# Attention in a fused block kernel: one running sum over all eight key blocks, a third buffer of upper keys, and four projections per area in halves

## The chip, the cores and the metric

The kernel runs on one core of one Trainium2 chip. The metric is the device time of one execution in microseconds. The core has a matrix engine (PE, with its weight loads shown apart as PEld), a vector engine (DVE), an activation engine (ACT), a general engine (POOL) and a queue engine (SP). ACT, POOL and SP can issue DMAs, which 16 DMA engines carry out. SBUF is the on-chip memory of 128 partitions; PSUM is the memory of eight banks per partition that PE writes.

## The reference, cut to what matters

The whole computation has two layers (an attention, a recurrence, convolutions with a state-space mixer, and a mixture of experts). The change touches the first part of layer 0 only, an attention over areas of the image. B = 2 images of 64 x 64 pixels with 256 channels are cut into four areas each; an area has 1024 pixels, and eight heads of 32 channels.

```python
qk = _conv1x1_bn(x, w_qk, qk_g, qk_b, qk_m, qk_v)
vv = _conv1x1_bn(x, w_v, v_g, v_b, v_m, v_v)
pp = conv_general_dilated(vv, w_pe, (1, 1), [(2, 2), (2, 2)], feature_group_count=C)
pp = _bn(pp, pe_g, pe_b, pe_m, pe_v)
...
attn = jnp.einsum('bhdn,bhdm->bhnm', q, k) * hd ** (-0.5)
attn = jax.nn.softmax(attn, axis=-1)
o = jnp.einsum('bhdm,bhnm->bhdn', v, attn)
...
return _conv1x1_bn(o + pp, w_proj, pr_g, pr_b, pr_m, pr_v)
```

The input of it is x, normalised over its channels, and the result is added to x. All is float32.

## The kernel before

**Tiling.** Eight areas (two images of four areas) are worked on one after the other. An area A has two groups of four heads, c = 0 and 1, so there are 16 groups G. A group has 1024 queries in two query halves n of 512, and 1024 keys in eight key blocks m of 128. The loop at L572 runs over 256 slots: slot t of a group (0 to 15) is query half n = t // 8 and key block m = t % 8. In tiles the four heads of a group lie on the 128 partitions for queries and keys (32 each).

**One slot** consists of, in the order in which the instructions are issued:

1. `scores` (L376): four matmuls of a bfloat16 row that subtracts each query's maximum (L381), then four matmuls of keys against queries (L386), into two PSUM tiles of two banks each. ACT takes the exponential of both into `exs[0]` and `exs[1]`, 128 x 1024 float32 each (L393). For m % 4 = 0 these tiles are named `sx0`, `sx1`, for the others `ex0`, `ex1`; each name has two buffers.
2. `values` (L403) of the slot before: four matmuls of the values against the exponentials (L399, `av_o`), summed over the eight key blocks in one PSUM bank.
3. `maxima` (L280) for the next group: four matmuls (L286). At even places ACT keeps the positive part of a product with the difference of upper and lower keys (`kd`, L298); at odd places DVE adds the product with the lower keys and takes the extreme value (L302), so that 1024 keys are searched in two products of 512.
4. The sum of exponentials, which the softmax divides by. It is not made from single key blocks: blocks are first added up on the 128 keys of a block. `total` is the pair of tiles of a block with m % 4 = 0. For the other blocks POOL issues a DMA that adds `exs[0]` into `total[0]` (L596); of `exs[1]` blocks 1 and 3 go by such a DMA (L602) and block 2 is added by POOL itself (L598), ordered behind the last matmul of `maxima` in that slot.
5. Other work of the same or neighbouring groups, from the tables `BEFORE`, `BEHIND`, `BEHIND_AREA`, `LATE` and `LATE_AREA` (L512 to L537), which name for each t a function, how many groups or areas ahead it works, and its arguments. `TAPS` says how many taps of the 5 x 5 depthwise convolution DVE does in each slot (L356).
6. Three slots after the fourth block of such a sum, `sums` (L414): four matmuls with a matrix of ones (L399, `po<-sx`) add up the 128 keys. After blocks 0 to 3 ACT keeps the result in `sum` (L421). After blocks 4 to 7 DVE adds `sum` and the new result (L425), turns it (L427), takes the reciprocal (L429), turns it back (L430) and multiplies the values (L433).

**Work from the tables** that the change moves: `query`, `key` (L260, L265: two matmuls of 512 columns by `project`, L157, and an ACT eviction with scale and bias), `v_half` (L227: the same for the values' image, and for half 0 two copies of border rows by POOL, L238 and L239), `v_tokens` (L241: four transposes on PE, one ACT copy), `output` (L366: projection and a DVE addition into x, L369), `mean_of_sum` and `variance_of_sum` (one 512-column product each, L172, and an ACT copy), `shift`, `centre`, `square`. Not moved are `root` (L203: at t = 6 a DVE transposition, at t = 7 POOL's power -0.5, L212 and L213), `join` (L308: four small POOL operations on the maxima, L318 and L319, at t = 11 and 15), `place` (L322: one matmul, an ACT copy, four DMAs from SP, L333, at t = 3 and 14) and `key_difference` (L271, at t = 15, L274).

**Order.** The order on every engine is the order of the program text (a manual schedule); the framework adds the semaphores that data and buffers need. A DMA that adds into a tile is issued by POOL after the DMA before it into the same tile has landed. PSUM has three tiles of two banks (`wide`, for scores and maxima), one bank `po` that all table work and the sums share, one use per slot, and one bank for `av_o`.

```python
tiles, k = [wide(), wide()], ks[G, m // HM]
...
exs.append(pe.tile([P, 2, 512], F32, name=f"{'ex' if m % 4 else 'sx'}{i}", bufs=2))
```

Of the kernel before, what the change touches and what calls it, by code (L numbers as in the profile page):

```python
# [10 lines left out]
F32 = mybir.dt.float32  # L11
# [3 lines left out]
ALU = mybir.AluOpType  # L15
# [3 lines left out]
P = 128  # L19
# [74 lines left out]
def area_attention(tc, sh, ap):  # L94
# [13 lines left out]
    with ExitStack() as ctx:  # L108
# [48 lines left out]
        def project(wt, c, src, half, out):  # L157

            for k in range(2):
                nc.tensor.matmul(  # L160
                    out, wt[:, k, c * P : (c + 1) * P], src(k)[:, HALVES[half]], start=k == 0, stop=k == 1
                )
# [61 lines left out]
        def columns(t):  # L224
            return lambda k: t[:, k]

        def v_half(A, c, half):  # L227

            if A not in vhs:
                vhs[A] = p2.tile([P, 2, AROWS + 4, WW], F32, name="vh")  # L230
            ps, r0 = bank(), 2 + half * AROWS // NQ
            project(w["wv"], c, columns(xns[A]), half, ps)
# [19 lines left out]
        def rows_of(wt, G, half, name, s, t, ps):  # L252
            A, c = GROUPS[G]
            ps = bank() if ps is None else ps
            project(wt, c, columns(xns[A]), half, ps)
            out = p2.tile([P, 512], F32, name=f"{name}{half}")
            nc.scalar.activation(out, ps, AF.Identity, scale=s[:, c : c + 1], bias=t[:, c : c + 1])
            return out

        def query(G, half, ps=None):  # L260
            if half == 0:
                nms[G] = p2.tile([P, NQ, GH, NM], F32, name="nm")
            qs[G, half] = rows_of(w["wq"], G, half, "q", s_qk, t_qk, ps)

        def key(G, half, ps=None):  # L265
            ks[G, half] = rows_of(w["wk"], G, half, "k", s_qk[:, 2:4], t_qk[:, 2:4], ps)
# [99 lines left out]
        def output(A, co, half):  # L366
            ps, to = bank(), area(A)[:, co, HALVES[half]]
            project(w["wpr"], co, lambda k: ys[A, k], half, ps)
            nc.vector.scalar_tensor_tensor(to, ps, s_pr[:, co : co + 1], to, ALU.mult, ALU.add)  # L369
# [6 lines left out]
        def scores(G, n, m):  # L376
# [37 lines left out]
        def sums(G, n, half, exs):  # L414
# [4 lines left out]
            if half == 0:  # L419
# [17 lines left out]
        with ExitStack() as own:  # L437
# [36 lines left out]
            query(0, 0, wide()[:, 0])  # L474
# [28 lines left out]
            for c in range(2):  # L503
# [10 lines left out]
            {0: [(1, query, 1)], 11: [(2, query, 0)], 13: [(2, key, 0)], 15: [(2, key, 1)]},  # L514
            {5: [(1, query, 1)], 9: [(2, query, 0)], 13: [(2, key, 0)], 15: [(2, key, 1)]},
# [16 lines left out]
                0: [(1, centre, 0)], 1: [(1, centre, 1), (1, square, 0)], 2: [(1, square, 1)],  # L532
# [7 lines left out]
        BEHIND_FIRST = {**BEHIND[0], 0: [(1, key, 1)]}  # L540
# [6 lines left out]
        for t in range(16):  # L547
# [3 lines left out]
            [2, 0, 1, 1, 2, 2, 2, 1, 2, 0, 0, 2, 3, 2, 3, 0],  # L551
            [4, 1, 1, 1, 3, 2, 3, 2, 2, 1, 1, 2, 2, 1, 2, 0],
# [19 lines left out]
        for g in range(16 * len(GROUPS)):  # L572
# [20 lines left out]
            if m % 4 == 0:  # L593
                total = exs
            if m % 4:
                nc.gpsimd.dma_start(total[0], exs[0], accum_op=ALU.add)  # L596
            if m % 4 == 3:
# [9 lines left out]
            works(G, t, BEHIND_FIRST if new else BEHIND[c], BEHIND_AREA[c])  # L607
# [7 lines left out]
            if m % 4 == 3:  # L615
                due[g + 3] = G, n, m // 4, total
# [1715 lines left out]
```

## Time and profile before

| | us |
|---|---|
| median of 3 runs (lowest, highest) | 2897.39 (2895.99, 2899.67) |
| the profiled execution | 2893.63 |
| span of its trace | 2891.8 |

| engine | busy us | share of the span | instructions |
|---|---|---|---|
| PE | 2631.5 | 91% | 17234 |
| PEld | 1483.3 | 51% | 17234 |
| DVE | 1963.8 | 68% | 3729 |
| ACT | 1554.5 | 54% | 2641 |
| POOL | 1239.8 | 43% | 1164 |

The rest of the profile is a page with slices of the span (each digit is the busy share of one fortieth of the span in tenths; PEclk is the granted clock of PE), the DMA queues, the chain of work that ended last, groups of instructions by line with their busy time and mean duration, and DMA issues. The trace behind it gives the order of time, the waits with what released them, and sums over stretches. In a row of the order of time stand start and duration in us, engine, line, operation, `out<-in`, shapes and a count; in brackets the idle time of the engine before it and what ended it. One float32 matmul of the program appears as two passes (x8 for four).

The groups that the change touches, each with count, busy us and mean ns: L596 DMA issue x192, 166.7, 868; L598 POOL addition x64, 171.8, 2684; ACT exponentials L393 `ex` x384, 376.1, 1029. In the chain that ended last, `PE po L399` has 2% of the span and `DMA sx<-ex` 3%. The queue of POOL's DMAs (q0) had its packets for 43.0% of 16 engines' span, and `sx<-ex` was issued 320 times with 512 KB each.

### The profile page before, as it was taken

The page shows a single profiled execution, that of the slowest core. Times are in us where ns is not written, and L with a number is a line of the kernel's source. Part 1 is how long each engine was busy: PE and PEld are TensorE (multiplying, and loading weights), DVE is VectorE, ACT ScalarE, POOL GpSimd, SP SyncE. Part 2 cuts the span into 40 slices and gives each one's busy share as a digit, 9 for nine tenths or more (in the row PEclk, how much of TensorE's full clock was granted, in tenths as well). Part 3 has the DMA queues.
Part 4 walks back from the last instruction along what each step waited for, and adds up shares of the span by engine and source line. Part 5 has one row for each costly group of instructions (what it writes and reads, how often), then busy time and mean ns, then how long its engine had stood idle before and what let it go on. Part 6 is the DMA issues. An engine that isn't in the chain of part 4 may idle for free.

```text
span 2891.8 us, 45886 instructions
## 1 busy us (share of the span) xinstructions
PE 2631.5 (91%) x17234; PEld 1483.3 (51%) x17234; DVE 1963.8 (68%) x3729; ACT 1554.5 (54%) x2641; POOL 1239.8 (43%) x1164
## 2 busy tenths in 40 slices
PE   7899999999999999997799999878885699999984
PEld 2223333333333333321699999833443588888873
DVE  5788879898888979786566667788887522222116
ACT  3567676666767676763344555576645522222223
POOL 1444545444444445443221000078771266666651
PEclk9999999999999999998899999989998899999995
DMA  3566666666676666767240000035553266666648
GB/s 132 110 128 126 129 128 131 126 132 131 128 137 132 132 132 127 138 130 144 90 175 1 2 1 1 9 99 150 142 136 122 87 235 221 229 225 227 229 171 342
DMA packets 104826, 388.16 MB, mean 134 GB/s; under 512 B 19656, under 2 KB 20560, under 8 KB 94864
## 3 DMA queue, kind: packets, MB, share of 16 engines
q0 software_dynamic: 71488, 293.00, 43.0%
q1 hardware_dynamic: 31872, 87.86, 9.4%
q10 hardware_dynamic: 1232, 4.25, 0.4%
q8 instruction: 138, 2.26, 0.3%
q14 instruction: 96, 0.79, 0.1%
HBM read 173.30 MB, written 43.58 MB: 75 GB/s over the span
## 4 chain that ended last, share of the span: by engine, by line
PE 73%; DVE 11%; issue 5%; DMA 4%; ACT 3%; POOL 3%; SPq 0%; ACTq 0%; DVEq 0%; POOLq 0%
PE ps L286 9%; PE ph L2078 9%; PE py L2088 8%; PE po L160 7%; PE av_o L399 7%; PE z L805 7%; PE z L817 7%; PE ps L386 6%; DMA sx<-ex 3%; PE ps L381 3%; PE yp L1560 2%; PE po L399 2%; DVE hs L1550 2%; DVE more L302 1%; DVE acc L356 1%
## 5 line engine op out<-in xcount | busy, mean ns | idle before, releaser
L356 DVE SCALAR_TENSOR_TENSOR acc<-vh,w_pe,acc 128x1008 f32<-128x1008 f32 (+7 forms) x384 | 529.5, 1382 | 9.1
L596 POOL DMA_DIRECT2D sx<-ex x192 | 166.7, 868 | 692.7 <-DMA sx<-ex 278.3
L393 ACT ACTIVATE ex<-ps 128x1024 f32<-128x1024 f32 x384 | 376.1, 1029 | 125.9 <-PE ps L386 50.4
L302 DVE CUSTOM_DVE_ANT_0 more<-ps,more 128x512 f32<-128x512 f32 x480 | 302.9, 687 | 133.5 <-PE ps L286 124.6
L2080 ACT ACTIVATE act<-ph,wt 128x256 f32<-128x256 f32 x272 | 128.8, 474 | 386.5 <-PE ph L2078 379.1
L2068 DVE COPY xt<-px 128x512 f32<-128x512 f32 x68 | 47.0, 692 | 396.5 <-PE px L2066 396.5
L2078 PE MATMUL ph<-xt,wt 128*128 128x256 f32 x1088 | 291.6, 391 | 5.0 <-ACT act L2080 3.0
L386 PE MATMUL ps<-q,k 32*128 32x512 f32 x2048 | 285.2, 602 | 0.0
L2088 PE MATMUL py<-wt,act 128*128 128x256 f32 x1088 | 278.7, 379 | 0.0
L298 ACT ACTIVATE more<-ps 128x1024 f32<-128x1024 f32 x240 | 233.4, 1028 | 26.8 <-issue 9.1
L2078 PEld LDWEIGHTS ph<-xt,wt 128*128 128x128 f32 x1088 | 190.4, 191 | 68.0 <-DVE xt L2068 24.0
L805 PE MATMUL z<-xs,u 128*128 128x128 f32 x1872 | 224.0, 277 | 0.0
L805 PEld LDWEIGHTS z<-xs,u 128*128 128x128 f32 x1872 | 217.7, 194 | 0.2 <-issue 0.2
L829 ACT ACTIVATE t<-z,bias 128x128 f32<-128x128 f32 x468 | 136.3, 361 | 145.1 <-PE z L817 145.1
L399 PE MATMUL av_o<-ex,vt 128*32 128x512 f32 x1536 | 212.0, 613 | 2.4 <-ACT ex L393 2.4
L2088 PEld LDWEIGHTS py<-wt,act 128*128 128x128 f32 x1088 | 201.6, 190 | 24.7
L2103 POOL DMA_INDIRECT results<-y,ri x136 | 138.0, 1014 | 138.9 <-DVE y L2096 115.6
L286 PE MATMUL ps<-k,q 32*128 32x512 f32 x1088 | 182.6, 639 | 1.7 <-DVE nm L292 1.3
L817 PE MATMUL z<-xs,v 128*128 128x128 f32 x1512 | 180.0, 275 | 0.1
L817 PEld LDWEIGHTS z<-xs,v 128*128 128x128 f32 x1512 | 174.2, 192 | 0.7 <-DVE xs L836 0.7
L598 POOL TENSOR_TENSOR sx<-sx,ex 128x1024 f32<-128x1024 f32 x64 | 171.8, 2684 | 4.7 <-PE ps L286 4.7
L1557 POOL TENSOR_TENSOR cs<-hs,cs 128x1024 f32<-128x1024 f32 x63 | 149.0, 2367 | 55.4 <-DVE hs L1550 33.8
(435 smaller groups left out, 4607.8 us busy)
## 6 DMA issues: line engine op xcount, KB each, us to landing
sx<-ex POOLq DMA_DIRECT2D x320, 512.0 KB
cs<-c_rows SPq DMA_DIRECT2D x128, 256.0 KB
y<-results SPq DMA_DIRECT2D x32, 512.0 KB
x<-xrows SPq DMA_DIRECT2D x8, 1024.0 KB
rows<-xt SPq DMA_DIRECT2D x16, 512.0 KB
out_x<-res POOLq DMA_DIRECT2D x15, 512.0 KB
xrows<-xn SPq DMA_DIRECT2D x24, 256.0 KB
x<-in_x SPq DMA_DIRECT2D x4, 1024.0 KB
```

The source lines that it names most:

```text
L160: nc.tensor.matmul(out, wt[:, k, c * P : (c + 1) * P], src(k)[:, HALVES[half]], start=k == 0, stop=k == 1)
L286: mm = nc.tensor.matmul(tiles[h // 2][:, h % 2], qs[G, i // HM][head(h), i % HM * P : (i % HM + 1) * P], keys[head(h)], start=True, stop=T ...
L298: nc.scalar.activation(held["more"][j], tiles[j], AF.Relu)
L302: nc.vector.tensor_tensor_reduce(more, tiles[h // 2][:, h % 2], more, -1.0, 3.0e38, ALU.add, ALU.min, accum_out=nms[G][:, 0, h, i : i + 1],)
L356: nc.vector.scalar_tensor_tensor(part, vh[:, c, 2 + r0 + dy : 2 + r1 + dy, w0 + dx : w1 + dx], w_pe[:, c, k : k + 1], part, ALU.mult, ALU.add,
L386: nc.tensor.matmul(tiles[h // 2][:, h % 2], k[head(h), m % HM * P : (m % HM + 1) * P], qs[G, n][head(h)], start=False, stop=True, tile_pos ...
L393: nc.scalar.activation(exs[i], tiles[i], AF.Exp, scale=HD**-0.5)
L399: nc.tensor.matmul(to[head(h)], lhs, exs[h // 2][:, h % 2], start=first, stop=last, tile_position=(0, HD * h))
L805: nc.tensor.matmul(z[c][:, g, :m], u[:, k, c, g], xt[:, k], start=g == GATES[0] and k == 0, stop=False, skip_group_check=True,)
L817: nc.tensor.matmul(z[c][:, g, :m], v[:, k, c, g], h[:, k], start=False, stop=k == 1, skip_group_check=True,)
L2078: nc.tensor.matmul(ph[:, hc], wt[:, at : at + P], xt[:, c], start=c == 0, stop=c == 1)
L2088: nc.tensor.matmul(py[:, j], act[:, hc, j * P : j * P + P], wt[:, at : at + C], start=hc == 0, stop=hc == NH - 1,)
```

## The change

1. The running sum goes over all eight key blocks of a query half. `total` is set at m = 0 only, `sx` tiles are used for m = 0 only and `ex` tiles for m = 1 to 7 (two buffers each, as before). `exs[0]` of blocks 1 to 7 goes into `total[0]` by DMA; of `exs[1]`, blocks 1, 3, 5 and 7 go by DMA and blocks 2, 4 and 6 are added by POOL. `sums` runs once per query half, three slots after m = 7, and DVE transposes its result straight from PSUM.
2. The upper half of the keys (`k1`) has three buffers, the lower half two. `key(2, 1)`, two groups ahead, moves from t = 15 to t = 11 (c = 0) or 9 (c = 1).
3. `query` and `output` can make one half of 256 columns at a time. Four calls per area are split: `query` of half 0 in both groups, and in the group c = 1 `query` of half 1 and the last `output`. The places in the tables where sums fell away are filled with these halves, and other table work moves by a few slots. The counts of taps per slot change.

```diff
         def sums(G, n, exs):
 
             ps = bank()
             for h in range(GH):
                 on_columns(ps, h, ones, exs, True, True)
-            if half == 0:
-                held["sum"] = p1.tile([P, 512], F32, name="sum")
-                nc.scalar.copy(held["sum"], ps)
-                return
-
-            y, total = ys[GROUPS[G]][:, HALVES[n]], held.pop("sum")
-            nc.vector.tensor_tensor(total, total, ps, ALU.add)
-            turned = exs[0][:, 0]
-            nc.vector.transpose(turned, total)
+            y, turned, total = ys[GROUPS[G]][:, HALVES[n]], exs[0][:, 0], exs[0][:, 1]
+            nc.vector.transpose(turned, ps)
...
-                exs.append(pe.tile([P, 2, 512], F32, name=f"{'ex' if m % 4 else 'sx'}{i}", bufs=2))
+                exs.append(pe.tile([P, 2, 512], F32, name=f"{'ex' if m else 'sx'}{i}", bufs=2))
...
-            if m % 4 == 0:
+            if m == 0:
                 total = exs
-            if m % 4:
+            else:
                 nc.gpsimd.dma_start(total[0], exs[0], accum_op=ALU.add)
-            if m % 4 == 3:
+            if m % 2 and m > 1:
                 add = nc.gpsimd.tensor_tensor(total[1], total[1], pending[3][1], ALU.add)
...
-            if m % 4 == 3:
-                due[g + 3] = G, n, m // 4, total
+            if m == NM - 1:
+                due[g + 3] = G, n, total
...
+        def columns_of(half, part):
+            return HALVES[half] if part is None else slice(512 * half + 256 * part, 512 * half + 256 * part + 256)
...
         def key(G, half, ps=None):
-            ks[G, half] = rows_of(w["wk"], G, half, "k", s_qk[:, 2:4], t_qk[:, 2:4], ps)
+            ks[G, half] = p2.tile([P, 512], F32, name=f"k{half}", bufs=2 + half)
+            rows_of(w["wk"], G, half, s_qk[:, 2:4], t_qk[:, 2:4], ks[G, half], ps, None)
...
-        def output(A, co, half):
-            ps, to = bank(), area(A)[:, co, HALVES[half]]
-            project(w["wpr"], co, lambda k: ys[A, k], half, ps)
+        def output(A, co, half, part=None):
+            at = columns_of(half, part)
+            ps, to = bank()[:, : at.stop - at.start], area(A)[:, co, at]
+            project(w["wpr"], co, lambda k: ys[A, k], at, ps)
...
         BEHIND = [
-            {0: [(1, query, 1)], 11: [(2, query, 0)], 13: [(2, key, 0)], 15: [(2, key, 1)]},
-            {5: [(1, query, 1)], 9: [(2, query, 0)], 13: [(2, key, 0)], 15: [(2, key, 1)]},
+            {
+                1: [(1, query, 1)], 11: [(2, key, 1)], 12: [(2, query, 0, 0)], 13: [(2, key, 0)],
+                15: [(2, query, 0, 1)],
+            },
+            {
+                4: [(1, query, 1, 0)], 6: [(1, query, 1, 1)], 9: [(2, key, 1)], 12: [(2, query, 0, 0)],
+                13: [(2, key, 0)], 15: [(2, query, 0, 1)],
+            },
         ]
         BEHIND_AREA = [
             {
-                1: [(0, v_tokens, 0, 1), (-1, shift, 0)], 3: [(0, v_tokens, 1, 0), (1, square_sum)],
-                4: [(1, variance_of_sum, 0)], 5: [(1, variance_of_sum, 1), (-1, shift, 1)], 7: [(-1, output, 0, 0)],
-                8: [(-1, output, 0, 1)], 9: [(-1, output, 1, 0)], 12: [(0, v_tokens, 1, 1)],
+                0: [(1, mean_of_sum, 1), (-1, shift, 0)], 3: [(0, v_tokens, 0, 1), (1, square_sum)],
+                4: [(1, variance_of_sum, 0)], 5: [(-1, output, 0, 0), (-1, shift, 1)],
+                6: [(1, variance_of_sum, 1)], 7: [(-1, output, 0, 1)], 8: [(0, v_tokens, 1, 0)],
+                9: [(-1, output, 1, 0)], 14: [(0, v_tokens, 1, 1)],
             },
             {
-                0: [(1, v_half, 0, 0)], 1: [(1, v_half, 1, 0)], 3: [(1, v_half, 0, 1), (2, mean_sum)],
-                4: [(2, mean_of_sum, 0)], 7: [(-1, output, 1, 1)], 8: [(2, mean_of_sum, 1)],
-                11: [(1, v_half, 1, 1)], 12: [(1, v_tokens, 0, 0)],
+                0: [(-1, output, 1, 1, 0)], 1: [(1, v_half, 0, 0)], 3: [(1, v_half, 1, 0), (2, mean_sum)],
+                5: [(-1, output, 1, 1, 1)], 7: [(1, v_half, 0, 1)], 8: [(2, mean_of_sum, 0)],
+                11: [(1, v_half, 1, 1)], 14: [(1, v_tokens, 0, 0)],
             },
         ]
...
         TAPS = [
-            [2, 0, 1, 1, 2, 2, 2, 1, 2, 0, 0, 2, 3, 2, 3, 0],
-            [4, 1, 1, 1, 3, 2, 3, 2, 2, 1, 1, 2, 2, 1, 2, 0],
+            [2, 0, 1, 0, 2, 1, 2, 2, 2, 0, 0, 2, 2, 2, 2, 0],
+            [3, 1, 1, 2, 2, 2, 2, 2, 3, 1, 1, 2, 3, 2, 3, 0],
         ]
```

More of the change, by code (lines that the diff above doesn't have):

```diff
@@ L155, in temp, with project @@
             return held[name, A]
-        def project(wt, c, src, half, out):
+        def columns_of(half, part):
+            return HALVES[half] if part is None else slice(512 * half + 256 * part, 512 * half + 256 * part + 256)
+        def project(wt, c, src, at, out):
             for k in range(2):
                 nc.tensor.matmul(
-                    out, wt[:, k, c * P : (c + 1) * P], src(k)[:, HALVES[half]], start=k == 0, stop=k == 1
+                    out, wt[:, k, c * P : (c + 1) * P], src(k)[:, at], start=k == 0, stop=k == 1
                 )
@@ L231, in v_half @@
             ps, r0 = bank(), 2 + half * AROWS // NQ
-            project(w["wv"], c, columns(xns[A]), half, ps)
+            project(w["wv"], c, columns(xns[A]), HALVES[half], ps)
             nc.scalar.activation(
@@ L250, in v_tokens, with rows_of, query @@
             nc.scalar.copy(vts[A, c][:, half * HM : half * HM + HM], blocks)
-        def rows_of(wt, G, half, name, s, t, ps):
+        def rows_of(wt, G, half, s, t, out, ps, part):
             A, c = GROUPS[G]
             ps = bank() if ps is None else ps
[L255 to L260, printed above, removed]
-            if half == 0:
-                nms[G] = p2.tile([P, NQ, GH, NM], F32, name="nm")
-            qs[G, half] = rows_of(w["wq"], G, half, "q", s_qk, t_qk, ps)
+            at = columns_of(half, part)
+            ps, to = ps[:, : at.stop - at.start], out[:, at.start - 512 * half : at.stop - 512 * half]
+            project(wt, c, columns(xns[A]), at, ps)
+            nc.scalar.activation(to, ps, AF.Identity, scale=s[:, c : c + 1], bias=t[:, c : c + 1])
+        def query(G, half, part=None, ps=None):
+            if not part:
+                if half == 0:
+                    nms[G] = p2.tile([P, NQ, GH, NM], F32, name="nm")
+                qs[G, half] = p2.tile([P, 512], F32, name=f"q{half}")
+            rows_of(w["wq"], G, half, s_qk, t_qk, qs[G, half], ps, part)
         def key(G, half, ps=None):
-            ks[G, half] = rows_of(w["wk"], G, half, "k", s_qk[:, 2:4], t_qk[:, 2:4], ps)
+            ks[G, half] = p2.tile([P, 512], F32, name=f"k{half}", bufs=2 + half)
+            rows_of(w["wk"], G, half, s_qk[:, 2:4], t_qk[:, 2:4], ks[G, half], ps, None)
         def head(h):
@@ L364, in add_taps @@
             nc.vector.tensor_tensor(y, y, accs.pop((A, c)).rearrange("p r w -> p (r w)"), ALU.add)
-        def output(A, co, half):
-            ps, to = bank(), area(A)[:, co, HALVES[half]]
-            project(w["wpr"], co, lambda k: ys[A, k], half, ps)
+        def output(A, co, half, part=None):
+            at = columns_of(half, part)
+            ps, to = bank()[:, : at.stop - at.start], area(A)[:, co, at]
+            project(w["wpr"], co, lambda k: ys[A, k], at, ps)
             nc.vector.scalar_tensor_tensor(to, ps, s_pr[:, co : co + 1], to, ALU.mult, ALU.add)
@@ L412, in values, with sums @@
                 nc.scalar.copy(ys[A, c][:, HALVES[n]], values_of[0])
-        def sums(G, n, half, exs):
+        def sums(G, n, exs):
             ps = bank()
@@ L418, in sums @@
                 on_columns(ps, h, ones, exs, True, True)
-            if half == 0:
-                held["sum"] = p1.tile([P, 512], F32, name="sum")
-                nc.scalar.copy(held["sum"], ps)
-                return
-            y, total = ys[GROUPS[G]][:, HALVES[n]], held.pop("sum")
-            nc.vector.tensor_tensor(total, total, ps, ALU.add)
-            turned = exs[0][:, 0]
-            nc.vector.transpose(turned, total)
+            y, turned, total = ys[GROUPS[G]][:, HALVES[n]], exs[0][:, 0], exs[0][:, 1]
+            nc.vector.transpose(turned, ps)
             small = p1.tile([P, 512 // 32], F32, name="small")
@@ L473, in area_attention @@
                 pass
-            query(0, 0, wide()[:, 0])
+            query(0, 0, None, wide()[:, 0])
             key(0, 0, wide()[:, 0])
@@ L531, in area_attention @@
             {
-                0: [(1, centre, 0)], 1: [(1, centre, 1), (1, square, 0)], 2: [(1, square, 1)],
+                1: [(1, centre, 0), (1, square, 0)], 2: [(1, centre, 1), (1, square, 1)],
                 4: [(-1, add_taps, 1)], 6: [(1, root, 0)], 7: [(1, root, 1)],
@@ L539, in area_attention @@
         BEFORE_FIRST = {0: [(1, query, 1)], 5: [(0, place, 1)], 14: [(1, place, 0)]}
-        BEHIND_FIRST = {**BEHIND[0], 0: [(1, key, 1)]}
+        BEHIND_FIRST = {**BEHIND[0], 0: [(1, key, 1)], 1: []}
+        BEHIND_AREA_FIRST = {**BEHIND_AREA[0], 0: []}
         LATE_FIRST = {0: [(1, key_difference)], 3: [(0, join, 1)], **LATE}
@@ L606, in area_attention @@
                     next(conv, None)
-            works(G, t, BEHIND_FIRST if new else BEHIND[c], BEHIND_AREA[c])
+            works(G, t, BEHIND_FIRST if new else BEHIND[c], BEHIND_AREA_FIRST if new else BEHIND_AREA[c])
             if g in due:
```

## The prediction

> **What bounds the kernel now.** I read the slices of the span first, then sums over the attention stage, then the order of time of one area, then the waits. Columns of the fifth line: stretch, length, busy time of PE, PE weight load, DVE, ACT, POOL, granted clock, DMA share, GB/s.
>
> ```profile
> span 2891.8 us, 45886 instructions
> ...
> PE   7899999999999999997799999878885699999984
> ...
> DVE  5788879898888979786566667788887522222116
> ...
> 60.39:1212.52 1152.13, 1119.80 (x7397) 351.34 (x7396) 975.37 (x1500) 793.53 (x920) 532.33 (x485) 1.00 0.68 128
> ```
>
> The change touches only the attention, slices 1 to 19. There PE is busy 97% at the full clock, DVE 85%, ACT 69%, POOL 46%, DMA engines 68%. PE sets the pace, slot by slot (a slot is one key block):
>
> ```profile
> 620.07 0.10 PEld L381 LDWEIGHTS <-ones_b 3*128 3x128 bf16 x4 [0.76 <-issue]
> ...
> 623.55 0.16 PEld L399 LDWEIGHTS po<-sx,ones 128*32 128x32 f32 x8 [0.76 <-issue]
> ...
> 624.55 0.10 PEld L381 LDWEIGHTS <-ones_b 3*128 3x128 bf16 x4 [0.84 <-issue]
> ...
> 628.03 0.30 PEld L160 LDWEIGHTS po<-xn,wq 128*128 128x128 f32 x2 [0.76 <-DVE sum L430]
> ...
> 629.95 0.10 PEld L381 LDWEIGHTS <-ones_b 3*128 3x128 bf16 x4 [0.76 <-issue]
> ```
>
> L381 opens a slot. 623.55 to 624.55: the four matmuls of a sum cost 1.00 us; 628.03 to 629.95: a projection costs 1.92. A slot with a sum is 4.48, so the bare slot is 3.48. An area has 32 slots, 16 projections, 8 sums, 4 means or variances (1.0) and 4 groups of transposes (0.54): 111.4 + 30.7 + 8 + 4 + 2.2 = 156 us of PE work. Measured, areas 1 to 6 take (1212.5 - 241.0)/6 = 161.9.
>
> Under this cover runs a second chain, on POOL and its DMA queue:
>
> ```profile
> 612.50 0.88 POOL L602 DMA_DIRECT2D sx<-ex  x1 [0.30 <-POOL sx L598]
> ...
> 614.82 6.36 POOL L213 TENSOR_TENSOR root<-root,minus_half 128x32 f32<-128x32 f32 x1
> 621.14 0.92 POOL L596 DMA_DIRECT2D sx<-ex  x1
> 621.76 1.21 POOL L602 DMA_DIRECT2D sx<-ex  x1
> 626.30 0.86 POOL L596 DMA_DIRECT2D sx<-ex  x1 [3.33 <-DMA sx<-ex]
> 631.65 0.85 POOL L596 DMA_DIRECT2D sx<-ex  x1 [4.49 <-DMA sx<-ex]
> 632.22 2.66 POOL L598 TENSOR_TENSOR sx<-sx,ex 128x1024 f32<-128x1024 f32 x1
> 635.17 0.87 POOL L602 DMA_DIRECT2D sx<-ex  x1 [0.30 <-POOL sx L598]
> ...
> 639.95 0.87 POOL L596 DMA_DIRECT2D sx<-ex  x1 [0.34 <-PE po L160]
> ```
>
> These are m = 1, 2, 3 of one sum. Every L596 adds into the same tile, so each waits until the one before has landed: 621.14, 626.30, 631.65. Then comes a pause, because m = 4 starts a new tile and issues nothing. The pause is what keeps this chain hidden. How long one DMA takes shows the DMA share (the last number but one) around the lone L602 of 635.17 and around the pair 639.95/640.52:
>
> ```profile
> 636.60:639.38 2.78, 2.78 (x16) 1.13 (x12) 2.71 (x4) 1.02 (x2) 2.56 (x3) 1.00 0.99 189
> 639.38:641.38 2.00, 1.60 (x13) 0.52 (x12) 2.00 (x7) 0.78 (x1) 1.65 (x3) 1.00 0.00 0
> 641.38:647.20 5.82, 5.82 (x49) 1.40 (x45) 5.68 (x7) 5.18 (x7) 1.18 (x2) 1.00 1.05 197
> ```
>
> It starts 1.43 us after its issue, fills all 16 engines for 2.78 and has landed at 4.2; two take 5.8, one behind the other.
>
> **The change, part by part.** *Sums once per query half.* 32 of 64 go. PE: 32 x 1.00 = -32 us on the path. ACT loses 32 copies (L421, 593 ns: 19 us), DVE 32 additions (L425, 685 ns: 22 us); neither bounds.
>
> *Halved projections.* Four per area, 28 in all (the last area has no successor). No row has a 512-wide product of this shape in 256 columns; the near row is L2078, 128x256: 291.6/1088 = 0.268 us a pass. Eight passes are 2.14 against 1.92: +0.22 each (between 0 and 0.3), +6 us. ACT gains 21 evictions, DVE 7; under 0.2 us each by L2080 (474 ns for 256 columns against 779 for 512), hidden.
>
> So PE work is 156 - 4 + 0.9 = 153 us per area, 38.2 per query half, -25 us in all.
>
> *Moved steps.* Each slot still has one user of the single PSUM bank. The second variance now stands in the slot whose DVE transposition reads it (t = 6): at most 1 us of DVE waiting in 7 areas, covered by a slot without reductions. Query, key and output keep their counts; SP's mask rows (L333) keep steps 3 and 14. The border copies of v (L238/L239, 1.3 us together) move behind the DMAs of m = 3; POOL is then late by 0.5 us, but the transfer would queue anyway. *Third upper-key buffer:* it only lets key(2,1) be written at t = 9 or 11 while two others are read. The key difference loses 0.2 us of waiting for ACT at t = 15; next is the POOL add of that slot.
>
> *The running sum.* POOL gets 32 more DMAs (0.87 us) and 32 more adds (2.69). More important, m = 4 no longer rests: seven L596 wait for each other. Call T1, T3, T5, T7 the issue of L596 at odd m.
> - T1 to T3 exists: 10.5 in this area; over other areas 10.5 or 11.5. I take 11.0.
> - T3 to T5 is new: L596 lands at +4.2, the next issue is at about +4.85. But L602 was issued at +3.55 (631.65 to 635.17), starts at +5.0, and the new L596 stands behind it: +5.0 + 5.6 = +10.6, plus 0.7 to the issue: 11.3. Bounds: 10.5 by T1 to T3, where the L602 goes earlier; 12 by its slower areas. T5 to T7 the same. T1 to T7: 33.6.
> - T7 to the next T1: the `ex` ring has two buffers and all seven blocks use it, so the exponential of m = 1 waits for L596(7): 4.2 + 1.03 + 0.5 = 5.8. After t = 7 of the first group of an area, POOL computes the root: 3.55 + 8.64 (612.50 to 621.14) = 12.2. After t = 15 it does join: 3.55 + 4.8 (635.17 to 639.95), up to 6.0 elsewhere: 8.6.
> - join at t = 11 used to fall into the pause; now L596 of m = 4 is behind it: +8.35 instead of +4.85, though it then goes alone: T5 is 2.0 later.
>
> An area: 4 x 33.6 + 12.2 + 5.8 + 2 x 8.6 + 2 x 2.0 = 173.6 us. That is above PE's 153, so **the chain is the new bound**; ACT waits on `ex`, PE on ACT. The ring lets ACT run at most two blocks ahead, so nothing is won back. Against 161.9: +11.7 in each of six areas, +70. The second group of area 0 (67.2 + 16.4 = 83.6 against 83.3): 0. First group of the last area (no root): 83.6 against 78.4, +5. Last group, without maxima and already bound by this chain (1301.71 to 1370.26, 68.5 us): 67.2 + 5.8 + 3.55 = 76.6, +8. First group, slowed by other things: -1. Sum **+82**: 2893.6 + 82 = 2976 for the profiled execution; the median shown is 3.8 above it, so 2979.
>
> **A rule against the row.** The Trainium skill, "DMA: Bandwidth & Descriptors", section "Anatomy of one DMA", gives for a DMA from GpSimd about 2.0 us plus bytes over 436e3 per us: 3.2 us for 512 KB, 1.2 of it moving. By that estimate L596 of m = 4 lands near +8, T3 to T5 is 8.7, a half some 31 to 37 us, and the chain stays under PE's 38.2: the time would be 2872. The trace has 2.78 us of moving for these accumulating DMAs, 4.2 to landing. I take the row. The same page (section "Rules for kernel authors") says an accumulate beside another access of the same bytes can lose data and must wait for the earlier DMA's semaphore, so this wait is not one that may be missing.
>
> **Rivals.**
> - *PE keeps the pace; faster.* If DMAs of both tiles overlapped, a pair of slots would take under 9.5 us and the whole -25 us shows: **2872**. For it: PE 97%, and in 1300 us of attention PE waited for these DMAs only 30 us (12.5 of matmuls, 17.8 of weight loads). Against it: the queue time above. It decides when T1 to T7 plus 9.8 us of mean boundary is under 38.2. Chance 0.09.
> - *DVE takes the gain.* The POOL add slows DVE's taps beside it: mean 1382 ns where undisturbed ones take 1.25 us, 384 times (50 us); L274 takes 1471 against 693 of L433 of the same size (12), the sums of two tiles (L187, L181) 2588 and 1858 against 1217 (14): some 76 us for 64 adds, 1.2 each. 32 more: 38 us. If all shows and the 22 us of L425 don't help: 2897 - 25 + 38 = **2910** (2890 to 2920). Against it: DVE at 85% with adds tied to the reductions, which read PSUM and aren't slowed. Chance 0.09.
> - *Chain and key difference.* The late add at t = 15 falls on L274 (up to 2.8 us in this trace), and the first maxima of 15 groups wait: 2979 + 15 x 2.7 = **3020**. Chance 0.07.
>
> **The numbers.** The forecast has 0.75, its own range by the bounds (31.5 to 35.5 for T1 to T7) 2920 to 3035. Range for 8 in 10: 2920 to 3025. A change under 0.2% (6 us) can't be told from none. Faster 0.10, within 0.2% 0.04, slower 0.86.
>
> **What would show it.** L596 x224, L602 x128, L598 x96, half the `po<-sx` matmuls. POOL's wait on `sx<-ex` well over today's 278 us; T3 to T5 near 11.3; areas near 174; PE busy near 90%, its weight loads and ACT's `ex` waiting for `sx<-ex`. Root and join directly ahead of late L596. If areas come out near 157 with PE still at 97%, the queueing step was wrong; if L356 grows and DVE passes 93%, the second rival holds.

## The result, and the profile after

The changed kernel takes **3067.97 us** (median of 4 runs, 3064.27 to 3070.23), the kernel before 2898.53 measured beside it: ratio 1.0583, 95% interval 1.0565 to 1.0601. That is 169 us more, where 82 were forecast.

The page of the changed kernel, lines that answer to those shown of before:

```profile
span 3062.1 us, 45663 instructions
...
PE 2713.4 (89%) x17090; PEld 1517.2 (50%) x17090; DVE 2022.2 (66%) x3704; ACT 1550.4 (51%) x2630; POOL 1341.2 (44%) x1228
...
PE   7988999999998999888779999987888489999994
...
PEclk9988999999999999999889999998999789999995
...
L400 ACT ACTIVATE ex<-ps 128x1024 f32<-128x1024 f32 x448 | 445.1, 1027 | 310.4 <-DMA sx<-ex 86.8
L604 POOL DMA_DIRECT2D sx<-ex x224 | 202.3, 903 | 748.0 <-DMA sx<-ex 335.9
...
L606 POOL TENSOR_TENSOR sx<-sx,ex 128x1024 f32<-128x1024 f32 x96 | 255.0, 2656 | 8.0 <-PE ps L292 7.7
```

L604, L606 and L610 are the DMA of tile 0, the POOL addition and the DMA of tile 1 (L596, L598, L602 before). Counts are as forecast: x224, x96. From the first slot to the last the attention takes 1464.9 us where it took 1297.5: **167 us, practically the whole loss, are there**. Stretches of six areas (1 to 6) with PE, PEld, DVE, ACT, POOL busy, granted clock, DMA share and GB/s, the first of before, the second of the changed kernel:

```profile
240.95:1212.50 971.55, 950.75 (x6309) 298.86 (x6308) 836.31 (x1286) 680.88 (x790) 459.01 (x417) 1.00 0.69 131
```
```profile
260.40:1363.70 1103.30, 1012.04 (x6215) 326.18 (x6214) 880.80 (x1268) 678.31 (x785) 534.73 (x464) 0.94 0.67 127
```

PE falls from 98% to 92%, and no other engine takes its place: DVE is at 80%, POOL at 48%, the DMA engines at 67%. When everything has slack, waits in turn are the bound. The waits (total, times, longest) name them, first of before from 100 to 1400 us, then of the changed kernel from 100 to 1500:

```profile
POOL sx L596 <- DMA sx<-ex: 278.3, 64, 6.4
...
ACT ex L393 <- DMA sx<-ex: 27.2, 20, 5.0
```

```profile
POOL sx L604 <- DMA sx<-ex: 318.4, 85, 6.8
...
DVE more L308 <- PE ps L292: 212.2, 96, 7.4
...
ACT ex L400 <- DMA sx<-ex: 73.6, 56, 5.2
ACT ex L400 <- POOL sx L606: 64.8, 35, 3.3
...
PEld ps L292 <- DVE kd L280: 26.7, 10, 3.8
...
ACT sq L201 <- DVE xn L198: 22.6, 12, 3.1
...
PE ps L292 <- DVE kd L280: 17.7, 10, 2.8
```

The first line is the row of seven: POOL waits for the landing of the DMA before. The third and fourth are the `ex` ring (the two buffers of each `ex` tile) that holds ACT back to it; before they were 27.2 and 4.1 us. The lines with kd and sq are two smaller waits. The waits for kd were there before, too (34.3 us in all against 44.4); those for sq are new, and the prediction had them at nothing.

### The profile page after: what moved, and what is told of

The parts are those of the page before. It is cut to its first block, busy times and chain, and to the rows that moved or that the text cites. A ratio compares the mean times of both kernels' runs of the same rounds, so it can differ in the third digit from the quotient of the medians.

```text
span 3062.1 us, 45663 instructions
## 1 busy us (share of the span) xinstructions
PE 2713.4 (89%) x17090; PEld 1517.2 (50%) x17090; DVE 2022.2 (66%) x3704; ACT 1550.4 (51%) x2630; POOL 1341.2 (44%) x1228
## 4 chain that ended last, share of the span: by engine, by line
PE 35%; DVE 7%; issue 4%; DMA 3%; POOL 2%; ACT 2%; SPq 0%; DVEq 0%; POOLq 0%; ACTq 0%
PE ph L2086 8%; PE py L2096 7%; PE z L813 6%; PE z L825 6%; DVE hs L1558 2%; PE yp L1568 2%; DMA sx<-ex 1%; PE px L2074 1%; DVE bn L1555 1%; ACT xt L1824 1%; DMA results<-y,ri 0%; DMA band<-in_w_square 0%; POOL sx L606 0%; PE two L956 0%; PE bn L1547 0%
## 5 line engine op out<-in xcount | busy, mean ns | idle before, releaser
L362 DVE SCALAR_TENSOR_TENSOR acc<-vh,w_pe,acc 128x1008 f32<-128x1008 f32 (+7 forms) x384 | 610.2, 1591 | 9.3
L400 ACT ACTIVATE ex<-ps 128x1024 f32<-128x1024 f32 x448 | 445.1, 1027 | 310.4 <-DMA sx<-ex 86.8
L604 POOL DMA_DIRECT2D sx<-ex x224 | 202.3, 903 | 748.0 <-DMA sx<-ex 335.9
L393 PE MATMUL ps<-q,k 32*128 32x512 f32 x2048 | 314.2, 651 | 0.0
L406 PE MATMUL av_o<-ex,vt 128*32 128x512 f32 x1792 | 270.6, 657 | 9.4 <-ACT ex L400 9.4
L606 POOL TENSOR_TENSOR sx<-sx,ex 128x1024 f32<-128x1024 f32 x96 | 255.0, 2656 | 8.0 <-PE ps L292 7.7
L292 PE MATMUL ps<-k,q 32*128 32x512 f32 x1088 | 204.6, 673 | 23.7 <-ACT ex L400 22.5
L388 PE MATMUL ps<-mx,ones_b 3*128 3x512 bf16 x1024 | 144.8, 403 | 53.2 <-ACT ex L400 24.5
L292 PE MATMUL ps<-kd,q 32*128 32x512 f32 x960 | 171.2, 653 | 22.3 <-DVE kd L280 17.7
```

The lines of the kernel that those rows point to most:

```text
L292: mm = nc.tensor.matmul(tiles[h // 2][:, h % 2], qs[G, i // HM][head(h), i % HM * P : (i % HM + 1) * P], keys[head(h)], start=True, stop=T ...
L362: nc.vector.scalar_tensor_tensor(part, vh[:, c, 2 + r0 + dy : 2 + r1 + dy, w0 + dx : w1 + dx], w_pe[:, c, k : k + 1], part, ALU.mult, ALU.add,
L393: nc.tensor.matmul(tiles[h // 2][:, h % 2], k[head(h), m % HM * P : (m % HM + 1) * P], qs[G, n][head(h)], start=False, stop=True, tile_pos ...
L406: nc.tensor.matmul(to[head(h)], lhs, exs[h // 2][:, h % 2], start=first, stop=last, tile_position=(0, HD * h))
L606: add = nc.gpsimd.tensor_tensor(total[1], total[1], pending[3][1], ALU.add)
```

## Experiments

Eighteen kernels. Ratios are to the kernel before, measured beside each.

| run | what it is | us | ratio (95%) |
|---|---|---|---|
| e1 | before + running sum alone | 3057.85 | 1.0531 (1.0501, 1.0562) |
| e2 | before + tables and halves alone | 2987.17 | 1.0285 (1.0253, 1.0316) |
| e3 | changed, m = 4 of tile 0 left out | 2961.04 | 1.0193 (1.0159, 1.0227) |
| e4 | changed, squares a slot later | 3035.65 | 1.0464 (1.0430, 1.0498) |
| e5 | before + running sum in two chains | 2945.59 | 1.0165 (1.0147, 1.0183) |
| e6 | changed, join on DVE | 3029.28 | 1.0451 (1.0433, 1.0468) |
| e7 | e5, join on DVE | 2938.09 | 1.0129 (1.0112, 1.0146) |
| e8 | e5 with tables and halves, squares a slot later | 2960.96 | 1.0214 (1.0195, 1.0233) |
| e9 | changed, root on DVE | 3060.79 | 1.0549 (1.0528, 1.0571) |
| e10 | e5, root and join on DVE | 2925.13 | 1.0087 (1.0070, 1.0103) |
| e11 | e8, root and join on DVE | 2941.21 | 1.0132 (1.0109, 1.0155) |
| e12 | before, root and join on DVE | 2901.33 | 0.9996 (0.9983, 1.0009) |
| e13 | before, late addition behind kd | 2895.66 | 0.9992 (0.9983, 1.0001) |
| e14 | e10, late addition behind kd | 2943.13 | 1.0157 (1.0144, 1.0170) |
| e15 | e11, late addition behind kd | 2946.03 | 1.0163 (1.0150, 1.0176) |
| e16 | changed, three parts mended | 2985.06 | 1.0289 (1.0273, 1.0305) |
| e17 | e16, m = 4 of tile 0 left out | 2903.59 | 1.0015 (1.0005, 1.0026) |
| e18 | before, third upper-key buffer, kd at t = 14 | 2886.56 | 0.9957 (0.9942, 0.9971) |

### Which part of the change costs

**e1** takes the running sum alone:

```diff
-exs.append(pe.tile([P, 2, 512], F32, name=f"{'ex' if m % 4 else 'sx'}{i}", bufs=2))
+exs.append(pe.tile([P, 2, 512], F32, name=f"{'ex' if m else 'sx'}{i}", bufs=2))
...
-            if m % 4 == 3:
+            if m % 2 and m > 1:
                 add = nc.gpsimd.tensor_tensor(total[1], total[1], pending[3][1], ALU.add)
```

> The kernel before with the running sum over eight blocks alone: tables, taps and key buffers stay as they were. Theory A (seven L596 in a row, each behind the landing of the one before, plus POOL's root and join between them, set the pace): nearly all of the loss is here, 3010 to 3050 us, areas near 178 to 183 us. Theory B (the moved table work is what hurts, above all ACT's squares that now stand directly behind DVE's centring): this kernel saves 32 us of PE and comes out at 2865 to 2900 us.

+153 us: with old tables and no halved projection nearly the whole loss is there, as theory A said, 8 us above its range.

**e2** takes the rest alone: halves and new places, with sums of four blocks and two key buffers.

> The changed kernel with the sum in two parts of four blocks again, with the moved table work, the halves and the new counts of taps kept (two key buffers, so key(2,1) is at t = 15 again and the halves of query stand at t = 11 or 9 and 12). Theory A: the chain has its pause back and the time is near the kernel before, 2895 to 2930 us (0.9 us more PE work per area, and the wait of the squares). Theory B: most of the loss stays, 3000 us or more.

+82 us, expected by neither side. Part of it is of its own making: with sums of four blocks kept, slots 6 and 14 have two users of the one `po` bank (in first groups medians of 6.9 and 7.0 us, where before has 4.9 and 4.5). Much of the rest is in slot 3 of the first group, 9.2 us (mean) where before has 4.2; e4 bears on it. e1 and e2 add up to more than the change (235 against 169). My reading is that they share cover: what delays a slot costs less where ACT waits for the chain anyway.

**e3** keeps the change and leaves one DMA out, that of tile 0 at m = 4, so that the row has its pause again (that block is missing from the sum of tile 0).

```diff
             if m == 0:
                 total = exs
-            else:
+            elif m != 4:
                 nc.gpsimd.dma_start(total[0], exs[0], accum_op=ALU.add)
```

> The changed kernel without the DMA that adds the first tile of key block 4 into the running sum (that block is left out of the sum for half of the heads). Everything else, PE work included, is the same. Theory A: the chain rests once per query half, T3 to T5 falls from 12 us (14.6 behind join) to about 9.6, areas fall from 186 to about 166 us, time 2890 to 2930 us. Theory B: one DMA of eleven changes little, 3040 us or more.

107 us less than the changed kernel, though 31 more than theory A had at most. The 32 DMAs left out have 2.78 us of moving each (89 us) on engines that were busy 67% of the time, so this run alone doesn't part the row from the volume.

**e5** keeps all DMAs, additions and matmuls of e1 and cuts the row: blocks 5 to 7 of tile 0 go into tile 0 of block 4, and one last DMA adds that into `total[0]`. Tile 0 of block 4 is then an `sx` tile, with three buffers, and no longer takes a place in the `ex` ring. To make room the joined maxima have one buffer.

```diff
+                exs.append(pe.tile([P, 2, 512], F32, name=f"{'sx' if m == 0 or m == 4 and i == 0 else 'ex'}{i}", bufs=3 if m % 4 == 0 and i == 0 else 2))
...
+            if m % 4 == 0:
+                part = exs[0]
...
-                nc.gpsimd.dma_start(total[0], exs[0], accum_op=ALU.add)
+                nc.gpsimd.dma_start(part, exs[0], accum_op=ALU.add)
...
+            if m == NM - 1:
+                nc.gpsimd.dma_start(total[0], part, accum_op=ALU.add)
```

> The sum-alone kernel, but the first tile's sum runs in two parts, blocks 0 to 3 and 4 to 7, each in a tile of its own (a third buffer for these tiles, paid for by single buffers of the rows of maxima), and one DMA behind block 7 adds the second part to the first. As many DMAs (352), POOL additions (96) and PE matmuls as in the sum-alone kernel; only the row of seven DMAs that wait for each other is cut. Theory A (the length of that row is the cost): areas fall from 183 to about 157 to 160 us and the time to 2860 to 2890 us, below the kernel before. Theory C (POOL's additional work or the number of DMAs is the cost, not their order): it stays above 3000 us.

112 us less than e1 with the same traffic. So most of the cost is **the row without a rest, not the volume** and not DVE beside 32 more additions, which e5 has too. The two ways in which the row acts, the wait of one DMA for the one before and the place of block 4 in the ring, were cut together and not apart. Theory A had e5 below the kernel before, and there it missed: 46 us stay. PE's saving doesn't show, since slots 6 and 14, bare without the sum (2.7 to 3.2 us), give it back in the slot behind (7.0). The excess over before is mostly slot 13 of the first group, 10.0 us (mean) where before has 5.8: 4.2 of the 5.3 us that an area is longer.

### What the rest is

The change also moves ACT's squares into the slot of DVE's centring of the same half (`LATE_AREA`):

```diff
-0: [(1, centre, 0)], 1: [(1, centre, 1), (1, square, 0)], 2: [(1, square, 1)],
+1: [(1, centre, 0), (1, square, 0)], 2: [(1, centre, 1), (1, square, 1)],
```

**e4** puts the squares one slot behind the centring again:

```diff
-1: [(1, centre, 0), (1, square, 0)], 2: [(1, centre, 1), (1, square, 1)],
+1: [(1, centre, 0)], 2: [(1, centre, 1), (1, square, 0)],
```

with `square(1)` in front of `square_sum` at t = 3.

> The changed kernel with ACT's two squares of the centred input one step later than DVE's centring, as in the kernel before (t = 2, and t = 3 ahead of the sum of squares). Theory A with this part counted apart: T1 to T3 in the first query half of an area falls from 14.3 to about 11 us, 3.3 us in each of 7 areas, 3040 to 3050 us. Rival: the chain waits at the next place instead, and the time stays within 5 us of 3068.

32 us less, 4 beyond theory A. ACT's and then DVE's order of time in the changed kernel, area 4, show why:

```profile
817.11 1.06 ACT L201 ACTIVATE sq<-xn 128x1024 f32<-128x1024 f32 x1 [0.55 <-DVE xn L198]
818.08 1.92 ACT L400 ACTIVATE ex<-ps 128x1024 f32<-128x1024 f32 x2
...
824.97 1.06 ACT L201 ACTIVATE sq<-xn 128x1024 f32<-128x1024 f32 x1 [3.14 <-DVE xn L198]
825.93 1.92 ACT L400 ACTIVATE ex<-ps 128x1024 f32<-128x1024 f32 x2
```
```profile
821.33 0.72 DVE L427 STREAM_TRANSPOSE sx<-po 128x512 f32<-128x512 f32 x1 [3.20 <-PE po L406]
...
823.72 1.22 DVE L198 TENSOR_TENSOR xn<-x,pm 128x1024 f32<-128x1024 f32 x1
```

The second square stands ahead of the exponential of m = 3 in ACT's queue and waits 3.14 us for a centring that stands behind the transposition of a sum (L427), which waits for PE. So L604 of m = 3 comes 14.3 us after that of m = 1, in e4 10.8 (means over areas 1 to 6).

**e6** puts `join` on DVE (`eng=nc.vector`).

> The changed kernel with the four small operations of each join on DVE instead of POOL. Theory A: T3 to T5 behind join at t = 11 falls from 14.6 us to about 12, the step from T7 to the next T1 behind t = 15 from 9.8 to 7 to 8 us; some 3 to 8 us per area, 3005 to 3045 us. Rival (join only fills a wait that is there anyway): within 5 us of 3068.

39 us less. POOL's order of time in the changed kernel around t = 11 of a second group:

```profile
960.60 0.86 POOL L604 DMA_DIRECT2D sx<-ex  x1 [5.74 <-issue]
...
964.74 1.52 POOL L324 CAST parts<-nm 128x16 bf16<-128x16 f32 x1
966.34 1.28 POOL L325 TENSOR_TENSOR rest<-nm,parts 128x16 f32<-128x16 f32 x1
967.68 1.22 POOL L324 CAST parts<-rest 128x16 bf16<-128x16 f32 x1
968.98 1.23 POOL L325 TENSOR_TENSOR parts<-rest,parts 128x16 bf16<-128x16 f32 x1
970.16 0.88 POOL L604 DMA_DIRECT2D sx<-ex  x1
975.92 0.86 POOL L604 DMA_DIRECT2D sx<-ex  x1 [4.89 <-ACT ex L400]
```

A lone DMA is followed by the next dependent issue 5.1 us later; here it is 9.6, and T3 to T5 is 15.3. With join on DVE the mean of that step falls from 14.7 to 11.8.

**e9** puts `root` on DVE instead of POOL's 6.3 us power: 15 small operations of the reciprocal square root.

> The changed kernel with the root of the variance (POOL's 6.4 us power and the addition before it, at t = 7) computed on DVE instead, by fifteen small operations of a Newton iteration. Theory A: the step from T7 to the next T1 in the first group of an area falls from 12.2 us to 7 to 8, 4 to 5 us in each of 7 areas, 3033 to 3045 us. Rival: the wait moves to the next place and the time stays within 5 us of 3068.

7 us less, with intervals that overlap, where theory A had 23 to 35. The step after the root falls from 12.2 to 7.3, but DVE's 15 operations stand ahead of its reductions, and the next half has T1 to T3 of 14.2 instead of 11.1 and T3 to T5 of 13.3 instead of 11.7. My reading is that the wait has changed engines.

**e16** mends three at once: e4, e6, and the key difference at t = 14, away from the addition of t = 15, which the third upper-key buffer allows.

```diff
-LATE = {11: [(1, join, 0)], 15: [(2, key_difference), (1, join, 1)]}
+LATE = {11: [(1, join, 0)], 14: [(2, key_difference)], 15: [(1, join, 1)]}
```

> The changed kernel with its row of seven kept, and three parts mended together: the squares a slot later (alone -32 us), join on DVE (alone -39 us), key difference at t = 14 instead of 15, which the third upper-key buffer allows. Nothing is left out. Theory (three separate waits, which add up): 3068 - 32 - 39 = 2997, less 5 to 25 for the key difference: 2970 to 2995, and what is left over before, 75 to 95 us, is the row of seven with its boundaries, close to the +82 forecast for it. Rival (the chain takes up what each mending frees, so that they don't add up): 3005 to 3030.

83 us less than the change: 32 + 39, and 12 left for the key difference, within the 5 to 25 expected. So nothing speaks against waits that add up, though no run of the changed kernel moved the key difference alone, and single runs of e16 lie up to 14 us apart. What stays is 86 us over the kernel before.

**e17** is e16 with the DMA of m = 4 left out as in e3.

> e16_after_parts (2985: changed kernel, squares later, join on DVE, key difference at t = 14) without the DMA that adds tile 0 of block m = 4, so that its row falls into rows of three as before. Left out: that block's share in the sum of exponentials, for tile 0. POOL's additions, PE's work, halved projections and third buffer stay. Theory (what is left of the loss in e16, 86 us, is the row of seven, and under it PE's saving waits): back to the time before or under it, 2875 to 2910, with areas of 155 to 163 us. Rival (part of those 86 us comes from the tables, the halves or the 32 more additions): 2920 to 2960.

81 of those 86 us go, as theory had it. So what the three parts don't explain is the row of seven (32 transfers are left out here, too; that volume isn't the cost rests on e5). PE's saving of 25 us still doesn't show: in the first group of an area slot 13 takes 10.0 us (median) where before has 5.8, since the exponential of m = 4 now stands in the `ex` ring behind the POOL addition that the root made late.

### Looking for a version that is faster

**e7, e8, e10, e11** combine two chains with join on DVE, with tables and halves, with both, and with root on DVE.

> The kernel with two chains and join on DVE. Theory A: POOL is no bound there any more, so it gains little over the kernel with two chains alone, 0 to 15 us.

> Two chains, with the changed kernel's tables, halves and taps in place of those of before (two key buffers, the squares one step behind the centring). PE has 0.9 us more work per area than with two chains alone, and its slots are of more even length. Theory A: it is within 20 us of the kernel with two chains, below the kernel before; if even slots matter it is the faster of the two.

> Two chains with the tables of before, root and join on DVE. Theory A: POOL is no longer late behind t = 7 and the 9.8 us slot at t = 13 of the first group falls to about 5.5, areas from 167 to 162 us, 2895 to 2915 us; what stays above the PE work of 152 are the slots without any filling work (t = 6 and 14), 1.3 us per pair. Rival (DVE is too full for fifteen more operations): no gain over 2940.

> Two chains with the changed kernel's tables and halves, root and join on DVE. Theory A: both the chain and the slots without filling work are gone, areas fall from 169 to about 158 to 162 us, 2870 to 2910 us; it may be the first of these kernels to reach the kernel before. Rival: the slots at t = 11 and 13 stay long, 2940 us or more.

All stay above before; the best, e10, by 24 us. e7 gained 7 us on e5, as expected; theory A had the other three below the kernel before or close to it, and missed. Root and join on DVE bring slot 13 back to 5.8 us in e10, but slot 9 of the first group goes from 5.3 to 7.9. Halved projections and new places gained nothing in these kernels (e8 15 us over e5, e11 16 over e10). My reading is that they fill slots whose length ACT and POOL set.

**e12** is the control: root and join on DVE in the kernel before.

> The kernel before with root and join on DVE and nothing else, as the control of the two above: its chain has pauses that cover root and join. Theory A: within 10 us of the kernel before, either way. If it is faster by more, POOL's lateness cost something there too.

No change: with the pause at m = 4, moving both off POOL gains nothing.

**e13, e14, e15** order the late addition behind the key difference.

```diff
+            if last_slot:
+                rest(key_difference(G + 2))
```

> The kernel before, but in slot t = 15 POOL's addition (and the DMA of tile 1 behind it) is ordered behind the key difference on DVE instead of behind the last maxima product; nothing is left out. Theory D (the late addition of t = 15 stretches the key difference, and the first maxima of a group wait for it; the trace of before has 19 us of weight loads waiting for kd): L274 falls from a mean of 1471 ns towards 700, and the time by 5 to 20 us: 2880 to 2895. Rival (that wait is covered by the lead of ACT and of the queue, or the later addition makes the chain of the next half late by as much): within 6 us of before, 2895 to 2905. In that case the key difference has no part in the loss of the change either.

> The running sum in two chains with root and join on DVE (as e10_two_chains_dve, 2925), and the addition of t = 15 behind the key difference. Theory D: the 22 and 12 us that PE still waits for kd there fall to under 10, and the time by 15 to 35 us: 2890 to 2910, at or under the kernel before. Rival (the wait is only moved to the next thing that is late, since nothing of PE's work is saved in the slots without table work): 2915 to 2925.

> As e14_two_chains_kd with the tables of the changed kernel, halved projections and third upper-key buffer among them (as e11_two_chains_halves_dve, 2941, and the addition of t = 15 behind the key difference). Theory D: 2905 to 2930, the same 10 to 35 us off. If the halved projections and the new places are worth what PE's work says (25 us), it would be under e14_two_chains_kd; theory from e8 and e11: it is above it by 10 to 20 us, for the squares behind the centring and PE's lower clock. Rival: unchanged at 2935 to 2945.

Before gains 3 us, not resolved. In e14 PE's wait for `kd` does fall from 35 us to 2.5 (between 241 and 1230), and yet the kernel is 18 us slower than e10: the addition and the DMA behind it come late for the next half, and ACT's wait for that addition rises from 7.2 us to 22.5 in the same stretch. The theory held for the wait and fell for the time. e15 is 5 us over e11, with intervals that overlap.

**e18** takes the third upper-key buffer and the earlier upper key into the kernel before, and no other part of the change. It moves the key difference to t = 14 and a query to t = 15, so that nothing on POOL becomes later; to make room the joined maxima have one buffer.

```diff
-{0: [(1, query, 1)], 11: [(2, query, 0)], 13: [(2, key, 0)], 15: [(2, key, 1)]},
+{0: [(1, query, 1)], 11: [(2, key, 1)], 13: [(2, key, 0)], 15: [(2, query, 0)]},
```

> The kernel before with one thing taken over from the change: a third buffer of upper keys, so that the upper key stands at t = 11 or 9 and the key difference at t = 14, away from the late addition of t = 15; the query that stood there goes to t = 15. To make room the joined maxima have one buffer instead of two. Nothing is left out. Theory: the 28 us that PE waits for kd between 241 and 1230 go, and no chain is touched (unlike e13_before_kd, where the addition itself became later): 2870 to 2892, faster than both kernels. Rival (that wait was covered by what follows, as e13_before_kd suggests, which lost 16 us of it and gained 3): 2893 to 2905.

**2886.56 us, 0.9957 (0.9942 to 0.9971): faster than both kernels.** The gain on the kernel before is 0.4%, small but outside its interval. The groups of DVE by line, before and e18 (count, busy, mean ns, idle before):

```profile
L274 DVE TENSOR_TENSOR kd<-k,k 128x512 f32<-128x512 f32 x15 | 21.3, 1419 | 3.2 <-ACT k L257 3.2
```
```profile
L274 DVE TENSOR_TENSOR kd<-k,k 128x512 f32<-128x512 f32 x15 | 10.3, 688 | 3.8 <-PE ps L286 3.3 <-ACT k L257 0.6
```

The operation takes half the time away from the addition, and PE's waits for `kd` (28.2 us between 241 and 1230 before) are gone. Of these 28 us, 11 show in the time.

## Why the prediction was wrong in size

Direction and cause held: the pause at m = 4 had hidden the chain, and without it the chain sets the pace. What failed are terms of the sum: the boundary from T7 to the next T1, the step, and the moved squares and PE's clock, both put at nothing. Means of areas 1 to 6, in us:

| step | forecast | changed | e16 |
|---|---|---|---|
| (c = 0, n = 0) T1 to T7; to the next T1 | 33.6; 12.2 | 38.4; 12.2 | 34.4; 12.2 |
| (0, 1) | 35.6; 8.6 | 35.0; 7.8 | 35.0; 7.7 |
| (1, 0) | 33.6; 5.8 | 34.6; 7.5 | 34.7; 7.0 |
| (1, 1) | 35.6; 8.6 | 37.9; 9.8 | 35.3; 7.8 |
| area | 173.6 | 183.2 | 174.1 |

- **Chain step of 11.0 to 11.3: held, a little short.** In e16, area 3, the issues of L604 are the cleanest picture of it (the first is m = 1):

```profile
653.58 0.92 POOL L604 DMA_DIRECT2D sx<-ex  x1
658.76 0.86 POOL L604 DMA_DIRECT2D sx<-ex  x1 [3.34 <-DMA sx<-ex]
664.58 0.86 POOL L604 DMA_DIRECT2D sx<-ex  x1 [4.97 <-DMA sx<-ex]
669.66 0.85 POOL L604 DMA_DIRECT2D sx<-ex  x1 [0.69 <-DMA sx<-ex]
675.92 0.85 POOL L604 DMA_DIRECT2D sx<-ex  x1 [5.41 <-issue]
681.03 0.85 POOL L604 DMA_DIRECT2D sx<-ex  x1 [0.66 <-DMA sx<-ex]
687.58 0.86 POOL L604 DMA_DIRECT2D sx<-ex  x1 [5.70 <-DMA sx<-ex]
696.45 0.86 POOL L604 DMA_DIRECT2D sx<-ex  x1 [4.45 <-PE av_o L406]
```

  11.0, 11.3 and 11.7, by the queueing that the prediction worked out. Over all of e16 a step is 11.6, +5.0 us an area over the 11.2 taken. The rule of the Trainium skill weighed there ("DMA: Bandwidth & Descriptors", "Anatomy of one DMA"; by its formula an estimate of 3.2 us to landing) would give steps of 8.7. The row was right; the next issue follows 5.1 us after a lone DMA's.

- **T7 to the next T1, 5.8: failed.** In e16, without join on POOL, it took 7.0 to 7.8. The prediction let it wait for the DMA alone. The last two rows above are 8.9 apart, and the second was released by PE's matmuls on the values of m = 0 (`PE av_o L406`), which read the very tile that this DMA adds into. Of the 18 boundaries without root in areas 1 to 6 of e16, PE released 16 (11 by `av_o`), ACT's exponential two, and a landing none. The kernel before had it, too: in each of these areas `PE av_o` released the first issue of (1, 1). The stretch 684 to 696 of e16 (PE, PEld, DVE, ACT, POOL, clock):

```profile
684.00:696.00 12.00, 11.99 (x76) 3.88 (x70) 7.72 (x16) 7.47 (x10) 4.12 (x3) 0.84 0.67 128
```

  PE is never idle. T1 needs PE's scores of m = 0 and 1 and the values of m = 0, some two slots of PE's work on. My reading is that while the chain paces, the ring and the three PSUM tiles hold PE level with it, so that PE has no slot in hand when the row ends; a longer ring wasn't tried. PE's clock at one half (below) explains a part only: the 14 of these boundaries with none of it inside or in the 3 us ahead have a mean of 7.0, the other four (the one shown among them) 9.1. In e16 the three boundaries without root cost +5.1 us an area over 5.8 each.

- **join: +2.0 at t = 11 twice and +2.8 at t = 15 twice, 9.6 an area: too much.** Taking it away brought 4.9 an area in e6 (183.9 to 179.0 from first slot to first slot). After t = 11 of c = 0 its four operations took 1.4 to 2.9 us and hid; after t = 11 of c = 1 they took 5.4, and the step grew by 2.9.

- **Moved steps at no cost: failed.** I had weighed the second variance, border copies and queues, and passed over `centre` and `square`, which the change puts into one slot in L539. It costs 3.5 us in T1 to T3 of every first half (14.3 against 10.8 in e4); e4 is 32 us shorter in all.

- **PE at its full clock: put at nothing, and failed.** The prediction had 153 us of PE work an area under the chain; PE was busy 168.7 of 183.9. In areas 1 to 6 of the changed kernel the trace has the clock at one half in 25 stretches of 3.4 or 6.8 us (436.2 to 443.0, for one), 126 us in all; before in one of 3.4 us, in e16 in 15 with 65 us. At half speed 126 us hold back at most 63 us of PE's work (an estimate), of the 132 us that these areas lost. How much of that ended on the path stays open.
- **Key difference, 15 x 2.7 = 40 as a rival: real, small.** L280's mean is 1711 ns (1419 before), and of e16's gain 12 us are left for its move.

- **First area, -1 and 0 for its two groups: failed.** They took 20 us more than before, in e16 4, so the three parts mended there are most of it.

In the sum for an area: the chain without join was forecast at 164.0 and measured 174.1 in e16; join, forecast 9.6, is 4.9; squares, forecast 0, 4.5: 183.5, where the changed kernel has 183.9. The total of e16 (+86 us) stands close to the forecast +82, but by luck: a chain forecast 10 us an area too short and a join put in at 9.6, where e16 has no join on POOL. So three terms of like size were too small by 5.1 (boundary), 5.0 (step) and 4.5 us an area (squares), and join was too large by 4.7. The clock is no further term of this sum: what it cost lies within the others.

**Rivals.** "PE keeps the pace" fell with e1: 32 us less PE work, and 153 us more. "DVE takes the gain" had its effect and not its consequence: the taps (L362) have a mean of 1591 ns where before has 1382, 80 us more over 384 of them, twice the 38 of the forecast; but DVE waits 212 us for the maxima of PE and is busy 80%, so it isn't the bound. "Chain and key difference" (3020) was right in kind, at about a third of its size; squares, which no rival had, and join, which the forecast had, were larger. Why the steps of e16 grow from a mean of 11.4 in areas 1 to 3 to 11.9 in areas 4 to 6 was not tried.

## What to carry to other kernels

When a change removes a rest from a chain of dependent transfers, price the chain by the queue it shares, and price the place where it restarts by the work of the engine that it had been holding back: here that engine, and no landing, released the restart. In a hand-written order, look at every pair of producer and consumer that comes to stand in one slot, on whichever in-order queue the consumer stands: what waits there holds everything behind it. A rest in a chain covers more than the chain (here root and join, by e12), so small costs that are nothing before can all show at once after.

## What the runs showed of the hardware

- **PE's granted clock fell in the kernels in which PE had to wait more**: over areas 1 to 6 it was 1.00 before, with PE idle for 21 us, 0.94 in the changed kernel with 91 us, and 0.97 in e16 with 59 us. A pass of the scores took longer in the changed kernel, in the last column but one (mean ns) of before and after:

```profile
L386 PE MATMUL ps<-q,k 32*128 32x512 f32 x2048 | 285.2, 602 | 0.0
```
```profile
L393 PE MATMUL ps<-q,k 32*128 32x512 f32 x2048 | 314.2, 651 | 0.0
```

  The Trainium skill ("TensorE: Matmul & The Clock Gate", "HAM oscillation — how this bites in real kernels") says that a PE gap of over some 3.4 us brings the half clock back. Shorter gaps were enough here: in 24 of the 25 falls no gap of PE in the 7 us ahead reached 3.4 us, and in two the longest was 1.1 us. No run here tried the clock by itself, so what it took of the loss stays open; in the stretch 684 to 696 above it was 0.84 with PE full.
- **A DVE operation with two inputs from SBUF is held up by nearly all of a POOL addition**: the key difference takes 685 ns alone and at most 3324 before, 2.64 us more, beside an addition of 2.69. In the changed kernel the longest takes 3553; both end 0.56 us after the addition. The Trainium skill ("SBUF — State Buffer", "SBUF: two separate sides") calls the shared port a lock held for the whole instruction, not a share of bandwidth; by a share of one half the operation would take at most 1.4 us, an estimate from the 685 ns.
